# Rotary attention in a four-layer network: the rotation made from the head-padded projections by a VectorE shuffle and GpSimd, and the division moved ahead of the first sums

## The chip, the cores and the metric

The kernel runs on one core of a Trainium2 chip. The metric is the device time of one execution in microseconds. The engines are TensorE (PE; its weight loads are listed as PEld), VectorE (DVE), ScalarE (ACT), GpSimd (POOL) and the queue of SyncE (SP), which issues the transfers.

## The reference

The network takes eight sequences of 256 tokens with 128 features, and runs four layers. Each layer is a feed-forward part (halved and added), an attention part (added) and the same feed-forward part again. All is in float32. The twelve stages are

```python
# layer 0: mixture of experts, softmax attention, mixture of experts
# layer 1: a small projection, an RWKV-6 scan, the small projection
# layer 2: six layers of local attention and MLP, softmax attention, the six layers again
# layer 3: mixture of experts, the attention below, mixture of experts
x = x + _L3_attn_ref(_layernorm(x, axis=-1), L3_attn_Wqkv, L3_attn_Wout, L3_attn_bout)
```

The attention of layer 3, which is the one changed, has 16 heads of 8 features. Its numerator uses rotated queries and keys, its denominator the ones that are not rotated:

```python
def _rotate(t, cos, sin):
    te, to = (t[..., 0::2], t[..., 1::2])
    re = te * cos - to * sin
    ro = te * sin + to * cos
    return jnp.stack([re, ro], axis=-1).reshape(t.shape)

q_rot = _rotate(q, cos, sin)
k_rot = _rotate(k, cos, sin)
num = jnp.exp(jnp.einsum('bhqd,bhkd->bhqk', q_rot, k_rot) * scale)
den = jnp.sum(jnp.exp(jnp.einsum('bhqd,bhkd->bhqk', q, k) * scale), axis=-1, keepdims=True)
attn = jnp.where(causal[None, None], num / den, 0.0)
y = jnp.einsum('bhqk,bhkd->bhqd', attn, v)
return y.transpose(0, 2, 1, 3).reshape(B, C, D) @ Wout + bout
```

## The kernel before

Activations lie as 128 features (partitions) by tokens. The eight sequences are worked in four units of two sequences (`NG = 4`, `T = 512` tokens). A stage takes one unit after the other. What ends a unit and begins its next stage (a residual, a layer norm) is cut into pieces on a queue, and `pump` emits the next piece wherever a stage has a slot for it.

An attention stage works in quads: four heads of one unit, 16 quads in all (4 units x 4 quads). The projections of a quad are padded, so that head j of the quad begins at partition 32 j and has 8 rows there. `attention` runs steps t = 0 to 17. In step t, quad t is projected (`project`), quad t-1 gets its scores and exponentials in four pairs (`pair`: one sequence and two heads each), and quad t-2 is weighed with the values (`weigh`), turned by transposes and divided (`divide`). `before` holds what is made once per unit, and the slots `next(pieces)` and `next(tail)` in a step take pieces: first those of `before` for the next unit, then those of the queue. The last step of a unit also has the `tail`, its output projection.

In attention stages every engine's instructions stay in the order in which the code names them (the class `_Ordered`), so a wait at the head of an engine's queue holds up all that is named later.

PSUM is split three ways. `two(...)` gives a tile of two banks out of three such tiles, which `pp` (projections), `ms` (scores of the rotated) and `ss` (scores of the plain) take in turn. `accp` has one bank for the weighed values (`av`). `ps()` gives the one bank named `bank`, which everything else uses: the values, the transposes of the division, the layer norms, the per-unit products, the output projection. A product into `bank` has to wait until the last reader of what stood in it is done.

In the version before, the rotation is made per unit, in the compact layout. `before` of `attn3` projects queries and keys without padding (`L3_wqk`), copies them (`a_t`), multiplies by a constant matrix of signs (`rot2`) to get the partner of each feature, and forms `a_t * cos` on GpSimd, the partner times sin on VectorE (both `a_y`) and their sum on GpSimd (`a_rot`). For each quad, `project` makes the padded plain projections (`a_qk`), and picks the quad's rotated rows by a product with a selection matrix `sel` (`a_rr`), both copied out of PSUM by VectorE.

`pair` ends with the sums of the plain exponentials (`a_n`) into `q.den`, on VectorE (tile `a_den`). `divide` makes four transposes into `bank`, the reciprocals `a_rec` on VectorE, and the quotient `a_ctx`, which reads `bank`. In the step the division stands behind pair 0:

```python
if q2:
    self.weigh(q2, 1, True)
    self.weighed(q2)        # a_av: VectorE copies av out of PSUM
if q1:
    pair(0, q1)             # scores, a_e and a_n on ACT, a_den on VectorE
if q2:
    self.divide(q2)
next(pieces, None)
```

At the start of the stage GpSimd clears three value buffers (`a_v`, in `value_rows`), one after the other. Both versions have these memsets.

Nearly all instructions of this stage carry the line of the recording helper, L300, in the profile, so they are told apart by their tiles.

Of the kernel before, what the change touches and what calls it, by code (L numbers as in the profile page):

```python
# [24 lines left out]
ALU = mybir.AluOpType  # L25
# [3 lines left out]
P = 128  # L29
B, S, D = 8, 256, 128  # L30
NB = 2
T = NB * S
NG = B // NB
NH = 16
DH = 8
# [17 lines left out]
def _constants():  # L53

    f = np.float32
    p = np.arange(P)
    c = {}
    c["ident"] = np.eye(P, dtype=f)
    c["mean"] = np.full((P, P), 1.0 / P, f)
    c["ones"] = np.ones((P, P), f)  # L60
    c["iota"] = np.tile(np.arange(E, dtype=f), (P, 1))
    c["krow"] = (p % 32 == DH).astype(f)[:, None]
    c["eps"] = np.tile(
        np.array([1e-5, 2e-5, 2.0**-64, 0.5 * SH * math.log(2.0)], f), (P, 1)
    )
    blk = (p[:, None] // 64 == p[None, :] // 64).astype(f)
    c["blkm"] = blk / f(64)

    z = np.zeros((P, 32), f)
    z[:64, :16] = 1.0  # L70
    z[64:, 16:] = 1.0
    c["hsum"] = z
    z = np.zeros((P, 4), f)
    for n, r in enumerate((32, 96, 48, 112)):
        z[r, n] = 1.0
    c["hpick"] = z

    r = np.zeros((P, P), f)
    for m in range(P):
        if m % 2 == 0:  # L80
            r[m + 1, m] = -1.0
        else:
            r[m - 1, m] = 1.0
    c["rot2"] = r

    sel = np.zeros((P, 4, P), f)
    for g in range(4):
        for j in range(4):
            for d in range(DH):
                sel[DH * (4 * g + j) + d, g, 32 * j + d] = 1.0  # L90
    c["sel"] = sel.reshape(P, -1)


    lev = [np.eye(P, dtype=f)]
    for i in range(7):
        n = 2**i
        q = p // n
        lev.append(((q[:, None] % 2 == 0) & (q[None, :] == q[:, None] + 1)).astype(f))
    c["lev"] = np.concatenate(lev, 1)

    c["cq"] = np.where(p[None, :] > p[:, None], f(NEG), f(0))
    c["ck"] = np.where(p[:, None] > p[None, :], f(NEG), f(0))
    one9 = np.zeros((P, 32), f)
    one9[:, DH] = 1.0
    c["one9"] = one9


    i, key = np.arange(32), np.arange(64)
    ok = (key[None, :] >= i[:, None]) & (key[None, :] <= i[:, None] + WIN)
    m = np.zeros((2, 2, 32, 2, 64), f)  # L110
    m[:, 0] = np.where(ok, f(0), f(LNEG))[:, None, :]
    m[:, 1, :, 0, :WIN] = LNEG
    c["lmask"] = m.reshape(P, -1)
    m = np.zeros((2, 2, 32, 4, 32), f)
    m[:, 0] = np.eye(32, dtype=f)[:, None, :]
    m[:, 1, :, 0] = np.eye(32, dtype=f)
    c["lrow"] = m.reshape(P, -1)

    half = np.arange(0, 64, 2, dtype=f)
    inv_freq = f(1.0) / f(10000.0) ** (half / f(64))  # L120
    t = np.arange(S, dtype=f)
    fr = t[:, None] * inv_freq[None, :]
    fr = np.concatenate([fr, fr], -1).T
    base = (half + f(0.4 * 64)) / f(1.4 * 64)
    sc = base[None, :] ** ((t - f(S // 2)) / f(WIN // 2))[:, None]
    sc = np.concatenate([sc, sc], -1).T
    two = lambda a: np.concatenate([_partners(a.T).T] * 2, 0).astype(f)

    sgn = np.where(p[:64, None] < 32, f(-1), f(1))
    c["qcos"] = two(np.cos(fr) * sc * f(8.0))  # L130
    c["qsin"] = two(np.sin(fr) * sc * f(8.0) * sgn)
    c["kcos"] = two(np.cos(fr) * (f(1.0) / sc))
    c["ksin"] = two(np.sin(fr) * (f(1.0) / sc) * sgn)

    i = np.arange(DH // 2, dtype=f)
    th = np.power(f(10000.0), f(-2.0) * (i - f(1.0)) / f(DH))
    ang = t[:, None] * th[None, :]
    per = lambda a: np.tile(np.repeat(a.T, 2, axis=0), (NH, 1)).astype(f)
    c["rcos"] = per(np.cos(ang))
    c["rsin"] = per(np.sin(ang))  # L140

    groups = {
        "c1": ("ident", "mean", "ones", "iota", "krow", "eps"),
        "cs0": ("cq", "ck"),
        "cs1": ("lev", "blkm"),
        "cs2": ("hsum", "hpick", "lmask", "lrow", "qcos", "qsin", "kcos", "ksin"),
        "cs3": ("rot2", "sel", "ck", "one9", "rcos", "rsin"),
    }
    return {n: {k: c[k].astype(f) for k in ks} for n, ks in groups.items()}

# [9 lines left out]
def _partners(w):  # L160

    w = np.asarray(w)
    return w.reshape(w.shape[:-1] + (2, 32)).swapaxes(-1, -2).reshape(w.shape)
# [16 lines left out]
def _layout(inp):  # L180

    g = {k: np.asarray(v) for k, v in inp.items()}
# [56 lines left out]
    for k in ("k", "v", "r", "g", "o"):  # L239
        w1["W" + k] = g["L1_attn_W" + k].T  # L240
    wq = g["L2_attn_w_qkv"]
# [6 lines left out]
    wq = g["L3_attn_Wqkv"]  # L248
    w3 = {
        "L3_wq": _pad_heads(wq[:, :D]),  # L250
        "L3_wk": _pad_heads(wq[:, D : 2 * D]),
        "L3_wqk": wq[:, : 2 * D],
        "L3_wv": wq[:, 2 * D :],
        "L3_wo": g["L3_attn_Wout"],
    }
    a, at = {}, {}
# [9 lines left out]
    w = g["L2_ffn_Wqkv"].reshape(DEPTH, P, 3, 4, 4, 64)  # L266
    w = np.concatenate([_partners(w[:, :, :2]), w[:, :, 2:]], 2)
# [41 lines left out]
class _Net:  # L309
# [582 lines left out]
    def rotated_quads(self):  # L892

        nc = self.nc

        def project(q):
            u = q.unit
            sel = self.get("sel", P * q.g, P)
            q.m = []
            for name, parts in (  # L900
                ("a_qk", ((self.get("L3_wq", P * q.g, P), u.xn), (self.get("L3_wk", P * q.g, P), u.xn))),
                ("a_rr", ((sel, u.rot[0]), (sel, u.rot[1]))),
            ):
                pp = self.two("pp")
                for n, (w, rhs) in enumerate(parts):
                    self.mm(pp[:, n, :], w, rhs)
                t = self.work(name, (P, 2, T), bufs=3)
                nc.vector.tensor_copy(t, pp)
                q.m.append(t)
            q.den = self.work("a_den", (P, 4, 4), bufs=3)  # L910

        def pair(i, q1):
            b, p = i // 2, i % 2
            qk, rr = q1.m
            r, n = self.two("ms"), self.two("ss")
            self.scores([
                (r, rr[:, 1, :], rr[:, 0, :], b, (2 * p, 2 * p + 1), "ck"),
                (n, qk[:, 0, :], qk[:, 1, :], b, (2 - 2 * p, 3 - 2 * p), None),
            ])
            q1.e[b, p] = self.soft(r, 384)  # L920
            e = self.work("a_n", (P, 2, T), bufs=3)
            self.act(e, n, AF.Exp, scale=1.0 / math.sqrt(DH))
            nc.vector.tensor_reduce(
                q1.den[:, 2 * b : 2 * b + 2, 2 - 2 * p : 4 - 2 * p].rearrange("p c j -> p j c"),
                e.rearrange("p j (c k) -> p j c k", c=2), AX.X, ALU.add)

        def step(q0, q1, q2, q3, pieces, tail):
            if q0:
                project(q0)
            else:  # L930
                self.pump()
            if q2:
                self.weigh(q2, 1, True)
                self.weighed(q2)
            if q1:
                pair(0, q1)
            if q2:
                self.divide(q2)
            next(pieces, None)
            if q1:  # L940
                pair(1, q1)
            next(tail if tail else pieces, None)
            if q1:
                pair(2, q1)
                self.weigh(q1, 0, True)
            if tail:
                next(tail, None)
            if q1:
                pair(3, q1)

        return step

# [52 lines left out]

    def attn3(self):
        def before(u):
            nc = self.nc
            self.values(u, self.get("L3_wv"), None)
            yield  # L1010
            u.rot = []
            for i in range(2):
                pp = self.ps()
                self.mm(pp, self.get("L3_wqk", D * i, D), u.xn)
                t = self.work("a_t")
                nc.vector.tensor_copy(t, pp)
                yield
                rp = self.ps()
                self.mm(rp, self.get("rot2"), t)
                seq = lambda a: a.rearrange("p (b s) -> p b s", b=NB)  # L1020
                tab = lambda k: self.get(k).unsqueeze(1).to_broadcast([P, NB, S])
                y1, y2 = self.work("a_y1"), self.work("a_y2")
                nc.gpsimd.tensor_tensor(seq(y1), seq(t), tab("rcos"), ALU.mult)
                nc.vector.tensor_tensor(seq(y2), seq(rp), tab("rsin"), ALU.mult)
                y = self.work(f"a_rot{i}")
                nc.gpsimd.tensor_tensor(y, y1, y2, ALU.add)
                u.rot.append(y)
                yield

        self.attention(self.rotated_quads, before, self.get("L3_wo"), self.get("L3_bout"), 2)  # L1030

# [747 lines left out]
```

## Time and profile before

| | |
|---|---|
| time before, median of 3 runs | 5578.49 us (5568.84 to 5580.77) |
| the profiled execution's own time | 5561.13 us |
| its span, first to last instruction | 5559.4 us |
| mean granted TensorE clock | 0.962 |
| busy: PE, DVE, ACT, POOL | 90%, 63%, 44%, 42% of the span |
| the last attention, from its first `a_v` to its last `x` | about 5085 to 5383 us of the span |

All times of single instructions and waits come from this one profiled execution. A row of a timeline gives the start in us from the span's start, the length in us, the engine, the line, the operation, the tile written and the tiles read, the shape and how many instructions were merged; in brackets stands how long the engine was idle before and what released it. A row of groups ends with busy us and the mean ns of one instruction, and the idle time before with what ended it. A row of waits gives the total, the number of times and the longest. A float32 product of 128x512 shows as two passes.

### The profile page before, as it was taken

What the parts mean: (1) busy time and instruction counts of PE and PEld (TensorE: products, weight loads), DVE (VectorE), ACT (ScalarE), POOL (GpSimd) and SP (SyncE); (2) the same over time, 40 slices, a digit from 0 to 9 for tenths busy, and PEclk for the clock granted to TensorE, in tenths of its full rate; (3) what the DMA queues carried; (4) which work ended last, traced back from release to release, by engine and by line L of the source; (5) the groups of instructions that cost most, each with busy time, mean ns of one, the idle gap of its engine ahead of it and who ended that gap; (6) DMA issues with size and microseconds to landing.
All of it is one profiled execution on the core that took longest, in us unless ns stands there. A gap on an engine that the chain in (4) does not pass through costs nothing.

```text
span 5559.4 us, 161655 instructions
## 1 busy us (share of the span) xinstructions
PE 5031.0 (90%) x73456; PEld 3009.9 (54%) x73456; DVE 3494.9 (63%) x5863; ACT 2440.1 (44%) x2947; POOL 2344.1 (42%) x1205
## 2 busy tenths in 40 slices
PE   9999997899899899988889899989998988899889
PEld 6755754455555555555544455555555555555446
DVE  4444446767767767776645676767767676645555
ACT  2233235444545444444434444545444444433442
POOL 0000022666666666666500666666666666501000
PEclk9999999999999999999989999999999999999999
DMA  1000000111111111111000011111111111000000
GB/s 67 1 1 1 1 1 23 30 35 39 35 40 33 39 34 42 34 35 34 26 23 1 27 38 37 36 40 33 39 34 42 34 35 35 27 34 1 1 1 8
DMA packets 58334, 149.55 MB, mean 27 GB/s; under 512 B 9649, under 2 KB 23858, under 8 KB 57394
## 3 DMA queue, kind: packets, MB, share of 16 engines
q1 hardware_dynamic: 57650, 139.21, 8.3%
q8 instruction: 578, 9.47, 0.7%
q14 instruction: 106, 0.87, 0.1%
HBM read 45.52 MB, written 1.05 MB: 8 GB/s over the span
## 4 chain that ended last, share of the span: by engine, by line
PE 72%; DVE 17%; ACT 6%; issue 4%; POOL 1%; DMA 0%; SPq 0%; DVEq 0%; ACTq 0%; POOLq 0%
PE mm L355 10%; PE pp L300 10%; PE sc L300 7%; PE vp L300 7%; PE e_o L355 6%; PE wo_acc L300 6%; PE bank L300 6%; PE ge L300 5%; DVE l_yr L300 5%; PE cx L300 4%; PE ms L300 3%; PE w_acc L300 2%; DVE l_yk L300 2%; DVE l_yq L300 2%; PE ct L300 2%
## 5 line engine op out<-in xcount | busy, mean ns | idle before, releaser
L300 POOL TENSOR_TENSOR l_yr<-l_yr,l_ksin 128x1024 f32<-128x1024 f32 x192 | 456.8, 2379 | 1024.0 <-DVE l_yr L300 1024.0
L300 PE MATMUL pp<-l_xs,wqkv 128*128 128x512 f32 x1536 | 718.6, 611 | 5.3 <-DMA wqkv<-in_f_wqkv 3.7
L300 ACT COPY l_v<-vp 128x1024 f32<-128x1024 f32 x192 | 194.4, 1013 | 859.3 <-PE vp L300 859.3
L300 ACT ACTIVATE l_sq<-pp 128x1024 f32<-128x1024 f32 x384 | 391.4, 1019 | 283.3 <-PE pp L300 283.3
L300 DVE STREAM_SHUFFLE l_yr<-pp 128x1024 f32<-128x1024 f32 x384 | 505.9, 1318 | 0.0
L300 POOL TENSOR_TENSOR l_e<-l_e,l_rq 128x1024 f32<-128x1024 f32 x192 | 365.7, 1905 | 331.1 <-DVE l_e L300 301.4
L355 PE MATMUL mm<-x,m 128*128 128x512 f32 x1024 | 475.4, 604 | 1.4 <-ACT e_a L387 1.4
L300 DVE TENSOR_REDUCE l_mx<-sc 128x16 f32<-128x1024 f32 x192 | 235.1, 1224 | 374.6 <-PE sc L300 374.6
L300 POOL TENSOR_TENSOR l_yq<-l_yq,l_yr 128x1024 f32<-128x1024 f32 x192 | 456.0, 2375 | 15.0
L300 POOL TENSOR_TENSOR l_yk<-l_yk,l_yr 128x1024 f32<-128x1024 f32 x192 | 453.1, 2360 | 15.1
L300 POOL TENSOR_TENSOR l_yr<-l_yr,l_qsin 128x1024 f32<-128x1024 f32 x192 | 455.1, 2370 | 0.0
L300 PE MATMUL cx<-l_w,l_at 64*32 64x65 f32 x12288 | 304.0, 235 | 148.7 <-ACT l_at L300 123.2
L300 PEld LDWEIGHTS pp<-l_xs,wqkv 128*128 128x128 f32 x1536 | 279.1, 192 | 291.6 <-issue 285.8
L300 PE MATMUL sc<-l_kp,l_yq 64*32 64x64 f32 x24576 | 326.2, 236 | 104.1 <-issue 103.2
L300 PE MATMUL vp<-wqkv,l_xs 128*128 128x256 f32 x1536 | 399.5, 404 | 6.5 <-issue 5.3
L355 PEld LDWEIGHTS e_o<-m,e_h 128*128 128x128 f32 x3072 | 362.9, 192 | 60.6 <-issue 60.1
L300 PEld LDWEIGHTS sc<-l_kp,l_yq 64*32 64x32 f32 x24576 | 277.5, 111 | 172.0 <-issue 170.8
L300 PEld LDWEIGHTS cx<-l_w,l_at 64*32 64x32 f32 x12288 | 261.5, 109 | 197.7 <-ACT l_at L300 137.5
L355 PE MATMUL e_o<-m,e_h 128*128 128x128 f32 x3072 | 363.5, 275 | 0.0
L300 PE MATMUL wo_acc<-l_ct,wo 128*128 128x512 f32 x768 | 358.0, 599 | 0.1
L300 PEld LDWEIGHTS vp<-wqkv,l_xs 128*128 128x128 f32 x1536 | 286.3, 196 | 61.0 <-issue 10.5
L300 PE MATMUL cx<-l_v,l_at 64*32 64x65 f32 x12288 | 309.3, 236 | 6.0 <-issue 6.0
(285 smaller groups left out, 9513.1 us busy)
## 6 DMA issues: line engine op xcount, KB each, us to landing
l_w<-l_v SPq DMA_DIRECT2D x192, 390.0 KB
wqkv<-in_f_wqkv SPq DMA_DIRECT2D x48, 384.0 KB
l_w<-l_v SPq DMA_DIRECT2D x192, 65.0 KB
wo<-in_f_wo SPq DMA_DIRECT2D x12, 512.0 KB
l_rt<-l_rn SPq DMA_DIRECT2D x384, 8.0 KB
m<-in_m_w SPq DMA_DIRECT2D x16, 256.0 KB
w<-in_f_w SPq DMA_DIRECT2D x12, 341.0 KB
w<-in_f_w SPq DMA_DIRECT2D x12, 192.0 KB
```

Of the source, the lines that this page charges most:

```text
L300: r = f(*args, **kw)
L355: self.nc.tensor.matmul(out, lhsT=lhsT, rhs=rhs, start=start, stop=stop)
```

## The change

Four things are edited, all in the last attention.

First, the constants. The matrices `rot2` and `sel` and the unpadded weights `L3_wqk` are no longer loaded. The tables `rcos` and `rsin` now have the padded layout (8 rows in each 32), and the sign of the rotation is in `rsin`.

Second, `before` of `attn3` makes only the values. The two unpadded projections, the two products with `rot2`, their copies and the elementwise operations around them are gone.

Third, `project` makes the rotation for each quad from the padded projections in PSUM: VectorE swaps neighbouring partitions by a shuffle (`a_yr`), VectorE multiplies the projections by cos (`a_rr`), GpSimd multiplies the shuffled ones by the signed sin and adds them onto `a_rr`. The copy of the plain projections (`a_qk`) moves from VectorE to ScalarE. `a_yr` has three buffers, as `a_qk` and `a_rr` have.

Fourth, `pair` returns its sums as a function to be called later. Pairs 1 to 3 call it at once; for pair 0 the step calls it after `divide`, so that on VectorE the division of quad t-2 stands in front of the first sums of quad t-1.

```diff
-        "cs3": ("rot2", "sel", "ck", "one9", "rcos", "rsin"),
+        "cs3": ("ck", "one9", "rcos", "rsin"),
...
         def project(q):
-            u = q.unit
-            sel = self.get("sel", P * q.g, P)
-            q.m = []
-            for name, parts in (
-                ("a_qk", ((self.get("L3_wq", P * q.g, P), u.xn), (self.get("L3_wk", P * q.g, P), u.xn))),
-                ("a_rr", ((sel, u.rot[0]), (sel, u.rot[1]))),
-            ):
-                pp = self.two("pp")
-                for n, (w, rhs) in enumerate(parts):
-                    self.mm(pp[:, n, :], w, rhs)
-                t = self.work(name, (P, 2, T), bufs=3)
-                nc.vector.tensor_copy(t, pp)
-                q.m.append(t)
+            pp = self.two("pp")
+            for n, w in enumerate(("L3_wq", "L3_wk")):
+                self.mm(pp[:, n, :], self.get(w, P * q.g, P), q.unit.xn)
+            qk, rr, yr = (self.work(n, (P, 2, T), bufs=3) for n in ("a_qk", "a_rr", "a_yr"))
+            nc.vector.stream_shuffle(yr, pp, [i ^ 1 for i in range(32)])
+            nc.vector.tensor_tensor(seq(rr), seq(pp), tab("rcos"), ALU.mult)
+            nc.scalar.copy(qk, pp)
+            nc.gpsimd.tensor_tensor(seq(yr), seq(yr), tab("rsin"), ALU.mult)
+            nc.gpsimd.tensor_tensor(rr, rr, yr, ALU.add)
+            q.m = qk, rr
...
-            nc.vector.tensor_reduce(
+            return lambda: nc.vector.tensor_reduce(
                 q1.den[:, 2 * b : 2 * b + 2, 2 - 2 * p : 4 - 2 * p].rearrange("p c j -> p j c"),
...
             if q1:
-                pair(0, q1)
+                sums = pair(0, q1)
             if q2:
                 self.divide(q2)
+            if q1:
+                sums()
             next(pieces, None)
             if q1:
-                pair(1, q1)
+                pair(1, q1)()
...
         def before(u):
             self.values(u, self.get("L3_wv"), None)
             yield
-            u.rot = []
-            for i in range(2):
-                pp = self.ps()
-                self.mm(pp, self.get("L3_wqk", D * i, D), u.xn)
-                t = self.work("a_t")
-                nc.vector.tensor_copy(t, pp)
-                yield
-                rp = self.ps()
-                self.mm(rp, self.get("rot2"), t)
...
-                nc.gpsimd.tensor_tensor(seq(y1), seq(t), tab("rcos"), ALU.mult)
-                nc.vector.tensor_tensor(seq(y2), seq(rp), tab("rsin"), ALU.mult)
-                y = self.work(f"a_rot{i}")
-                nc.gpsimd.tensor_tensor(y, y1, y2, ALU.add)
-                u.rot.append(y)
-                yield
```

More of the change, by code (lines that the diff above doesn't have):

```diff
@@ L76, in _constants @@
     c["hpick"] = z
[L78 to L91, printed above, removed]
     lev = [np.eye(P, dtype=f)]
@@ L137, in _constants, with per @@
     ang = t[:, None] * th[None, :]
-    per = lambda a: np.tile(np.repeat(a.T, 2, axis=0), (NH, 1)).astype(f)
-    c["rcos"] = per(np.cos(ang))
-    c["rsin"] = per(np.sin(ang))
+    def per(a, sgn):
+        z = np.zeros((4, 32, S), f)
+        z[:, :DH] = np.repeat(a.T, 2, axis=0) * sgn[:, None]
+        return z.reshape(P, S)
+    even = np.arange(DH) % 2 == 0
+    c["rcos"] = per(np.cos(ang), np.ones(DH, f))
+    c["rsin"] = per(np.sin(ang), np.where(even, f(-1), f(1)))
     groups = {
@@ L251, in _layout @@
         "L3_wk": _pad_heads(wq[:, D : 2 * D]),
-        "L3_wqk": wq[:, : 2 * D],
         "L3_wv": wq[:, 2 * D :],
@@ L894, in rotated_quads @@
         nc = self.nc
+        seq = lambda a: a.rearrange("p n (b s) -> p (n b) s", b=NB)
+        tab = lambda k: self.get(k).unsqueeze(1).to_broadcast([P, 2 * NB, S])
         def project(q):
-            u = q.unit
-            sel = self.get("sel", P * q.g, P)
-            q.m = []
-            for name, parts in (
-                ("a_qk", ((self.get("L3_wq", P * q.g, P), u.xn), (self.get("L3_wk", P * q.g, P), u.xn))),
-                ("a_rr", ((sel, u.rot[0]), (sel, u.rot[1]))),
-            ):
-                pp = self.two("pp")
-                for n, (w, rhs) in enumerate(parts):
-                    self.mm(pp[:, n, :], w, rhs)
-                t = self.work(name, (P, 2, T), bufs=3)
-                nc.vector.tensor_copy(t, pp)
-                q.m.append(t)
+            pp = self.two("pp")
[8 more added lines that the diff above has]
+            q.m = qk, rr
             q.den = self.work("a_den", (P, 4, 4), bufs=3)
@@ L935, in step @@
             if q1:
-                pair(0, q1)
+                sums = pair(0, q1)
             if q2:
                 self.divide(q2)
+            if q1:
+                sums()
             next(pieces, None)
             if q1:
-                pair(1, q1)
+                pair(1, q1)()
             next(tail if tail else pieces, None)
             if q1:
-                pair(2, q1)
+                pair(2, q1)()
                 self.weigh(q1, 0, True)
@@ L948, in step @@
             if q1:
-                pair(3, q1)
+                pair(3, q1)()
         return step
@@ L1007, in before @@
         def before(u):
-            nc = self.nc
             self.values(u, self.get("L3_wv"), None)
             yield
-            u.rot = []
-            for i in range(2):
-                pp = self.ps()
-                self.mm(pp, self.get("L3_wqk", D * i, D), u.xn)
-                t = self.work("a_t")
-                nc.vector.tensor_copy(t, pp)
-                yield
-                rp = self.ps()
-                self.mm(rp, self.get("rot2"), t)
-                seq = lambda a: a.rearrange("p (b s) -> p b s", b=NB)
-                tab = lambda k: self.get(k).unsqueeze(1).to_broadcast([P, NB, S])
-                y1, y2 = self.work("a_y1"), self.work("a_y2")
-                nc.gpsimd.tensor_tensor(seq(y1), seq(t), tab("rcos"), ALU.mult)
-                nc.vector.tensor_tensor(seq(y2), seq(rp), tab("rsin"), ALU.mult)
-                y = self.work(f"a_rot{i}")
-                nc.gpsimd.tensor_tensor(y, y1, y2, ALU.add)
-                u.rot.append(y)
-                yield
         self.attention(self.rotated_quads, before, self.get("L3_wo"), self.get("L3_bout"), 2)
```

## The prediction

> **What bounds the kernel now.** I read the page first, for the whole program.
>
> ```profile
> span 5559.4 us, 161655 instructions
> PE 5031.0 (90%) x73456; PEld 3009.9 (54%) x73456; DVE 3494.9 (63%) x5863; ACT 2440.1 (44%) x2947; POOL 2344.1 (42%) x1205
> ```
>
> TensorE is busy for 90% of the span, but that average runs over twelve stages. The change touches the last attention only. By its tiles that runs from 5085 us (first `a_v`) to 5383 us (last `x`): about 298 us, 5.4% of the span. Nothing outside can move, apart from two constant loads that get smaller (0.46 MB of 149.55 MB, landed long before). So the second view is the waits, and the third the groups by shape, both from 5090 to 5385 us.
>
> ```profile
> ACT a_e L300 <- PE ms L300: 154.3, 52, 29.5
> DVE a_den L300 <- ACT a_n L300: 93.0, 59, 3.1
> PEld bank L300 <- DVE a_ctx L300: 39.4, 14, 3.1
> PE bank L300 <- DVE a_ctx L300: 35.6, 14, 2.8
> ```
>
> ```profile
> L300 PE MATMUL pp<-a_rot,sb_cs 128*128 128x512 f32 x64 | 30.1, 592 | 0.0
> L300 PE MATMUL bank<-a_t,sb_cs 128*128 128x512 f32 x16 | 14.4, 997 | 10.1 <-DVE a_ctx L300 8.5 <-issue 0.8 <-DVE a_t L300 0.8
> ```
>
> ACT and DVE mostly wait for others, so PE is the bound, and PE has one large wait of its own: 14 times, 35.6 us in all, it stands before a product into `bank`, because the division (`a_ctx`) has not yet read that one PSUM bank. The timeline of a step shows why.
>
> ```profile
> 5119.73 1.98 PE L300 MATMUL pp<-x,sb_w 128*128 128x512 f32 x4
> 5121.39 1.22 DVE L300 TENSOR_REDUCE a_den<-a_n 128x4 f32<-128x1024 f32 x1 [0.97 <-ACT a_n L300]
> 5121.56 1.88 PE L300 MATMUL pp<-a_rot,sb_cs 128*128 128x512 f32 x4
> 5122.52 1.21 DVE L300 COPY a_qk<-pp 128x1024 f32<-128x1024 f32 x1
> 5123.65 1.21 DVE L300 COPY a_rr<-pp 128x1024 f32<-128x1024 f32 x1
> 5124.78 0.68 DVE L300 COPY a_av<-av 128x512 f32<-128x512 f32 x1
> 5125.55 0.66 PE L300 MATMUL bank<-sb_c,a_av 128*128 128x128 f32 x4
> 5127.20 1.22 DVE L300 TENSOR_REDUCE a_den<-a_n 128x4 f32<-128x1024 f32 x1 [1.74 <-ACT a_n L300]
> 5128.69 0.29 DVE L300 TENSOR_TENSOR a_ctx<-bank,a_rec 128x128 f32<-128x128 f32 x1
> 5129.03 2.08 PE L300 MATMUL bank<-a_t,sb_cs 128*128 128x512 f32 x2 [2.82 <-DVE a_ctx L300]
> ```
>
> The transposes end at 5126.2, but DVE's queue has the sums of pair 0 (`a_den`, which needs ACT's exponential) in front of the division, so PE idles 2.82 us. The first product after it took 2.08 us for two passes, against 1.12 at other places: the clock had dropped.
>
> **The change part by part.** I count from the start of `pp` in a step (5119.73 is 0). Where two DVE rows follow each other, the distance of their starts counts (1.13 us for a 128x1024 copy).
>
> *Division ahead of the first sums.* The division no longer waits for `a_n`. Behind `a_av` come `a_rec` (0.24) and `a_ctx` (0.29), which needs the end of the transposes; then the sums. PE resumes some 0.1 us after `a_ctx`. The sums of pair 0 are read only by the next step's division, and `a_n` has three buffers: nothing is late by them.
>
> *The products of the rotation.* Per quad two selection products go (4 passes, 0.43 us each: 1.71 us), per unit two projections and two rotations (3.43 us); 16 x 1.71 + 4 x 3.43 = 41 us of PE. Not all of this lies on the path. In the step above PE reaches the transposes when DVE has made `a_av`, and that stands behind `a_den` of pair 3 and two 128x1024 passes. With the change the two passes are a shuffle and a product, which the long local stage already runs in this shape. Groups of the page (busy us, mean ns):
>
> ```profile
> L300 DVE STREAM_SHUFFLE l_yr<-pp 128x1024 f32<-128x1024 f32 x384 | 505.9, 1318 | 0.0
> L300 POOL TENSOR_TENSOR l_yr<-l_yr,l_qsin 128x1024 f32<-128x1024 f32 x192 | 455.1, 2370 | 0.0
> ```
>
> and, by tile (shortest, median and longest ns),
>
> ```profile
> L300 DVE TENSOR_TENSOR l_yq<-pp,l_qcos x192: 1193/1206/1225, 970.2 to 4833.4; 128x1024 f32<-128x1024 f32 x192
> L300 ACT COPY l_v<-vp x192: 1012/1012/1016, 975.0 to 4845.2; 128x1024 f32<-128x1024 f32 x192
> ```
>
> So DVE runs `a_den` 1.66, shuffle 2.79, product 4.00 (the local stage has 1.21 from a shuffle's start to the next row's), `a_av` 5.13 to 5.81; transposes at 5.90 instead of 5.82. PE, meanwhile, needs 1.71 for `pp`, 0.79 for the weighing, 1.40 for pair 0, and stands ready at 3.90. **The 1.71 us saved on the selection turn into a new 2.0 us wait for `a_av`**; this term is -0.08 x 14 = -1.1 us. After the transposes: `a_ctx` ends at about 6.9, PE resumes at 7.0 instead of 9.30 if a product into `bank` is next, else goes on with pair 1 at 6.40. In the new order of PE, a product into `bank` follows the division directly in 6 of the 14 steps (fewer pieces are left to spread), each waiting about 0.6 us. So of 35.6 us about 3.6 stay: **+32.0 us**.
>
> *Pieces.* From the third step on, nine of the per-unit products (the last of unit 1, all of units 2 and 3) go: 9 x 0.86 = **+7.7 us**; their copies on DVE (`a_t`, `a_y`, 0.69 each) were off the path.
>
> *The start.* Before, unit 0's chain of product, copy, product, product runs with nothing beside it, and pair 0 begins at 5110.24. Now the first `pp` can start when the values' products end (5085.42). DVE first copies `a_v` (done 5088.55, behind POOL's first memset), then shuffle and product to 5091.0; POOL's three memsets (5.34 us from 5085.98) end at 5091.3, then 2.38 + 2.36 for the two POOL passes: rotated projections at 5096.1, pair 0 at 5096.2. That is 14 us earlier; I take off 1 us since PE stands idle from about 5092 and begins at half clock. **+13 us**.
>
> *What is added beside the path.* ACT copies `qk` at about 2.0 to 3.0; its last exponential ends at 1.62 and the next, queued behind the copy, cannot start before 3.80, so it costs nothing; without that gap it would be 1.0 us a step. POOL makes 2 x 2.37 after the shuffle (4.1): `rr` is ready at about 8.9, and its first reader is pair 0 of the next step, at 11.9 + 2.5 = 14.4, since a step without pieces comes to about 11.9 us. Nothing else is queued on POOL. The PSUM buffer of `pp` is read until 5.1 and taken again by pair 1 at 6.40. SP only issues the two smaller loads.
>
> [...] *Clock.* Windows of 1 us around that step give
>
> ```profile
> 5128.00:5129.00 1.00, 0.00 (x0) 0.00 (x0) 0.88 (x3) 0.00 (x0) 0.00 (x0) 0.95 0.00 0
> 5129.00:5130.00 1.00, 0.97 (x1) 0.50 (x2) 0.00 (x0) 0.00 (x0) 0.00 (x0) 0.50 0.00 0
> 5132.00:5133.00 1.00, 1.00 (x17) 0.59 (x10) 0.00 (x0) 0.16 (x1) 0.95 (x1) 0.84 0.00 0
> ```
>
> (the seventh number is the granted clock). After a gap of 2.82 us the clock is 0.50 for about 3.4 us. Of three gaps of 1.53 us (ending at 5220.3, 5288.8 and 5302.7) the last did it, the others not. [...] The new gap of 2.0 us (then 0.6 more in six steps) lies nearer to 2.82 than to no gap, so I expect about as many cold windows as before: 0, with bounds of +15 and -5 (three more windows, 1.7 us each).
>
> [...]
>
> **Sum.** 32.0 + 7.7 + 13 - 1.1 = 51.6; I say 52. The profiled execution took 5561.1 us (its span and 1.7); the median shown is 5578.5, 0.3% longer. The same difference on the median: **5526 us**.
>
> **Rivals.**
> - *Clock kept.* If 2.0 us gaps leave the clock alone, 52 + 15 = 67: 5511 us. For it: one 1.53 us gap did nothing; and two more like it; against: eleven 2.82 us gaps, nearly all cooled. Chance 0.20.
> - *Start or pieces give less.* If the first steps stay cold, or layer norms queue behind the moved sums and PE waits for `bank` there, some 20 us of the gain go: 5546 us. Chance 0.17.
> - *Slower: POOL late.* If GpSimd's two passes were held up so that `rr` comes after 14.4, every pair 0 waits. The point is 4.1 + 2p = 14.4, p = 5.1 us a pass against 2.37 measured; to lose the whole gain and 11 us over 15 steps, lateness must reach 4.2 us: p = 7.3. At p = 8 it is 5.8 x 15 = 87 - 52 = 35 us slower: 5613 us. [...] Chance, with the unforeseen, 0.06.
> - *No visible change.* The gains eaten by new waits, 5570 to 5590: 0.04.
>
> The forecast itself has 0.53. About 0.2% (11 us) is what a measurement of this kernel can tell from no change; its three runs lie 12 us apart. Faster 0.90, same 0.04, slower 0.06. The range takes in the clock's bound with some run noise below and the small-gain case above: 5499 to 5549.
>
> **What would show it.** Right: waits for `a_ctx` at a few us; a wait of PE for `a_av` near 2.0 us in most steps, about 28 us in all; `ms<-a_rr` first at about 5096; the stage about 246 us long; granted clock there still 0.90 to 0.93. Wrong: waits of `ms` for POOL `a_rr` after the first step; `a_yr` on POOL above 5 us; a granted clock near 1.0 (more gain), or shuffles far from 1.32 us.

## The result, and the profile after

The changed kernel takes 5523.26 us (median of four runs, 5514.1 to 5532.29), and the kernel before 5573.66 us over the runs beside it. The ratio is 0.9913, with a 95% interval of 0.9891 to 0.9935: about 50 us faster, where 52 were forecast.

The page of the changed kernel begins:

```profile
span 5524.2 us, 161509 instructions
PE 5007.5 (91%) x73360; PEld 3006.1 (54%) x73360; DVE 3489.0 (63%) x5863; ACT 2452.8 (44%) x2963; POOL 2396.6 (43%) x1221
```

The two profiled spans differ by 35 us only. To see why, I take the stage by itself, from GpSimd's first clearing of `a_v` to the end of the last `x<-bank,sb_pv,x`. Before it runs from 5085.98 to 5383.52 (297.5 us), after from 5102.38 to 5348.22 (245.8 us): **51.7 us shorter**. What follows takes 176 us in both. What comes before the stage took 16.4 us longer in this one execution, though its instructions are the same in both kernels. So executions differ elsewhere by such amounts, and the stage is the sharper measure. I give it for each experiment, beside the runs. It comes from one profiled execution per kernel; two executions of the changed kernel gave 245.8 and 242.7 us. In experiments 1, 2, 3, 5 and 6 the interval of the runs' ratio overlaps with that of the changed kernel, so there the difference from the changed kernel rests on the stage.

PE's wait for `a_av` in the stage before (total, times, longest):

```profile
PE bank L300 <- DVE a_av L300: 2.4, 2, 1.9
```

The waits of the stage after the change (5103 to 5348 us):

```profile
ACT a_qk L290 <- DVE a_rr L290: 62.3, 16, 9.0
PE bank L290 <- DVE a_av L290: 25.5, 16, 1.9
PE ms L290 <- POOL a_rr L290: 4.4, 1, 4.4
PE bank L290 <- DVE a_ctx L290: 2.3, 6, 0.4
```

The 35.6 us for `a_ctx` have gone to 2.3. In their place stands `a_av` with 25.5, where it had 2.4 before, and GpSimd's result is waited for once, at the very start. A step of the timeline has the same order of events that the prediction walked through:

```profile
5210.81 1.98 PE L290 MATMUL pp<-x,sb_w 128*128 128x512 f32 x4
5212.47 1.22 DVE L290 TENSOR_REDUCE a_den<-a_n 128x4 f32<-128x1024 f32 x1 [2.24 <-ACT a_n L290]
5213.61 1.30 DVE L290 STREAM_SHUFFLE a_yr<-pp 128x1024 f32<-128x1024 f32 x1
5214.80 1.21 DVE L290 TENSOR_TENSOR a_rr<-pp,sb_cs 128x1024 f32<-128x1024 f32 x1
5215.92 0.68 DVE L290 COPY a_av<-av 128x512 f32<-128x512 f32 x1
5216.10 1.01 ACT L290 COPY a_qk<-pp 128x1024 f32<-128x1024 f32 x1 [3.67 <-DVE a_rr L290]
5216.66 1.02 PE L290 MATMUL bank<-sb_c,a_av 128*128 128x128 f32 x4 [1.69 <-DVE a_av L290]
5217.73 0.29 DVE L290 TENSOR_TENSOR a_ctx<-bank,a_rec 128x128 f32<-128x128 f32 x1 [0.96 <-PE bank L290]
5218.07 2.07 PE L290 MATMUL bank<-sb_w,x 128*128 128x128 f32 x8 [0.39 <-DVE a_ctx L290]
5218.77 1.22 DVE L290 TENSOR_REDUCE a_den<-a_n 128x4 f32<-128x1024 f32 x1 [0.76 <-ACT a_n L290]
```

Counted from `pp`, the shuffle begins at 2.80 (forecast 2.79), the cosine product at 3.99 (4.00), `a_av` at 5.11 (5.13), the transposes at 5.85 (5.90). PE resumes at 7.26 (7.0). One row is not where it was put: ScalarE copies `qk` at 5.29 instead of 2.0: it stands idle for 3.67 us until VectorE's `a_rr` is done, which reads the same PSUM tile. Experiment 6 asks what that costs.

Groups of the stage after (busy us, mean ns) show that the added passes cost what the local stage had shown:

```profile
L290 POOL TENSOR_TENSOR a_rr<-a_rr,a_yr 128x1024 f32<-128x1024 f32 x16 | 37.6, 2353 | 1.3
L290 DVE STREAM_SHUFFLE a_yr<-pp 128x1024 f32<-128x1024 f32 x16 | 20.8, 1299 | 0.0
L290 DVE TENSOR_TENSOR a_rr<-pp,sb_cs 128x1024 f32<-128x1024 f32 x16 | 19.3, 1208 | 0.0
L290 ACT COPY a_qk<-pp 128x1024 f32<-128x1024 f32 x16 | 16.2, 1012 | 62.3 <-DVE a_rr L290 62.3
```

Last, the windows over the stage (length, busy PE, PEld, DVE, ACT, POOL, then the granted clock, DMA share, GB/s), of before

```profile
5086.00:5383.00 297.00, 248.94 (x1969) 127.97 (x1970) 155.34 (x182) 118.64 (x142) 25.62 (x19) 0.90 0.00 1
```

and of after:

```profile
5103.00:5348.00 245.00, 206.49 (x1873) 113.49 (x1872) 145.53 (x181) 133.33 (x158) 79.90 (x35) 0.88 0.00 1
```

Read in slices of 0.2 us, the stage after the change has a clock of 1.00 or 0.50 in 1208 of 1230 slices; the other values stand where it changes. So a mean of 0.90 over 297 us is about 60 us at half clock, and 0.88 over 245 us is 59. The change left that amount as it was. This number decides most of what follows.

### The profile page after: what moved, and what is told of

It reads as the page before. It is cut to its first block, busy times and chain, and to the rows that moved or that the text cites. A ratio compares the mean times of both kernels' runs of the same rounds, so it can differ in the third digit from the quotient of the medians.

```text
span 5524.2 us, 161509 instructions
## 1 busy us (share of the span) xinstructions
PE 5007.5 (91%) x73360; PEld 3006.1 (54%) x73360; DVE 3489.0 (63%) x5863; ACT 2452.8 (44%) x2963; POOL 2396.6 (43%) x1221
## 4 chain that ended last, share of the span: by engine, by line
PE 71%; DVE 17%; ACT 6%; issue 4%; POOL 1%; DMA 0%; DVEq 0%; SPq 0%; POOLq 0%; ACTq 0%
PE mm L345 10%; PE pp L290 9%; PE vp L290 7%; PE sc L290 7%; PE e_o L345 6%; PE wo_acc L290 6%; PE bank L290 5%; PE ge L290 5%; DVE l_yr L290 4%; PE cx L290 4%; PE ms L290 2%; PE w_acc L290 2%; DVE l_yk L290 2%; PE ct L290 2%; DVE l_yq L290 2%
```

## The experiments

My theory has three parts. VectorE's queue, not TensorE's work, sets when a step goes on. Where TensorE is made to stand still for some 1.7 us in each step, the clock falls to half for 3.41 or 6.83 us (in the stage after it is at half for no other length), so a gap costs more than its length. GpSimd's passes are hidden. The rivals are that the removed TensorE work is the gain, that ScalarE's new wait lies on the path, and that the clock does not mind such gaps.

### 1. The division edit alone

```diff
 # the kernel before, and only this of the change:
-                pair(0, q1)
+                sums = pair(0, q1)
             if q2:
                 self.divide(q2)
+            if q1:
+                sums()
```

> The kernel before with the fourth edit alone (sums of pair 0 behind the division). My theory: the 14 waits of PE for a_ctx (35.6 us) shrink to about 0.6 us each, since the transposes still end near 6.5 us of a step and a_ctx then follows at once: 27 us off, and the clock about as it was; stage (first values product to last x) 298 to about 271 us. Rival (the products are what counts, the wait only moves to the next thing, ACT or PSUM): under 10 us off, other waits of PE grow by what a_ctx loses. Second rival (with the 2.8 us gaps gone, the clock also stays up): 27 + 15 = 42 us off.

Measured: 5512.44 us against 5556.58 for the kernel before on this chip, ratio 0.9913 (0.9898 to 0.9928); the stage 250.4 us, 47 shorter. Its wait for `a_ctx`, and its windows:

```profile
PE bank L300 <- DVE a_ctx L300: 4.2, 11, 0.4
...
PE bank L300 <- DVE a_av L300: 2.4, 2, 1.9
```

```profile
5073.00:5322.00 249.00, 230.89 (x1969) 118.84 (x1970) 154.43 (x181) 117.71 (x142) 24.85 (x19) 0.97 0.00 1
```

The second rival holds. The wait shrank by 31 us, and the clock rose from 0.90 to 0.97 as well, from about 60 to 15 us at half clock. One call moved behind another, with no work removed, gives 47 of the 52 us that the whole change gives, and by the runs the same ratio.

### 2. The rotation alone

```diff
 # the changed kernel, with the sums of pair 0 called at once:
-                sums = pair(0, q1)
+                pair(0, q1)()
             if q2:
                 self.divide(q2)
-            if q1:
-                sums()
```

> The changed kernel with the sums of pair 0 called at once, in front of the division: edits one to three alone. My theory: the start keeps its 12 us and the pieces their 8; the wait for a_av stays near 1.7 us a step; but the division comes behind a_n again, which is now late (ACT copies qk at 5.3 and makes a_n until 8.0), so a_ctx ends at about 9.7 and the six steps with a product into bank behind the division wait 2.5 us and more, and the tails' transposes too: about 20 us of the 50 go, 30 off against before. The two edits alone (27 + 30) then give about what both give together. Rival (all gain is from removed TensorE work, the division edit adds nothing): 50 off, as the changed kernel.

Measured: 5523.2 against 5556.58, ratio 0.9938 (0.9925 to 0.9952); the stage 266.2 us, 31 shorter than before, as expected. PE now has both waits, and the lowest clock so far:

```profile
PE bank L290 <- DVE a_av L290: 25.5, 16, 1.9
PE bank L290 <- DVE a_ctx L290: 21.4, 9, 3.3
```

```profile
5080.00:5345.00 265.00, 212.04 (x1873) 116.18 (x1872) 145.53 (x181) 133.33 (x158) 79.55 (x35) 0.84 0.00 1
```

The stage gains 47 by the one part, 31 by the other, and 52 by both. So the parts do not add. Against the kernel with the division edit alone, the rotation brings only 5 to 8 us more (250.4 to 245.8 and 242.7), which the runs do not show, though it takes 41 us of TensorE work away: it also brings the wait for `a_av`, and with it the low clock.

### 3. One more VectorE pass in front of `a_av`

```diff
-            nc.scalar.copy(qk, pp)
+            nc.vector.tensor_copy(qk, pp)
```

> The changed kernel with the copy of the plain projections back on VectorE, behind shuffle and cosine product: one more pass of 1.13 us in front of a_av. My theory (VectorE's chain a_den, shuffle, product, a_av sets when the transposes start): PE's wait for a_av grows from 1.7 to 2.8 us, 14 to 15 steps x 1.1 = 16 us slower than the changed kernel, with the clock a little lower. Rival (ScalarE, which now waits for VectorE before it copies, is the bound): moving the copy off ScalarE makes it no slower or faster.

Measured: 5525.79 against 5556.58, ratio 0.994 (0.9925 to 0.9956); the stage 263.6 us, 18 longer than the changed kernel's (16 expected).

```profile
PE bank L290 <- DVE a_av L290: 41.1, 16, 2.8
```

```profile
5077.00:5340.00 263.00, 212.42 (x1874) 115.81 (x1873) 162.51 (x197) 118.60 (x142) 80.21 (x35) 0.85 0.00 1
```

The wait grew from 25.5 to 41.1 us. This is VectorE's chain, seen from the other side: the 16 passes of 1.13 us in front of `a_av`, 18 us in all, are paid in full. The clock fell from 0.88 to 0.85, but little is left over that it could have cost. ScalarE was relieved of the copy and that helped nothing.

### 4. Useless products in the gap

```diff
         tp = self.ps()
+        if q.den is not None:
+            for _ in range(4):
+                self.mm(tp[:, :S], self.get("ident"), self.get("rcos"))
         for c in range(4):
```

> The changed kernel with four useless products (each 128x256, two passes, 1.7 us in all at full clock) into the bank of the transposes just in front of them, where PE otherwise waits some 1.7 us for a_av; what they write is overwritten. My theory (gaps of 1.7 us cool the clock for a window of 3.4 us or two): the granted clock in the steps rises from 0.89 to over 0.95, and the stage gets 10 to 18 us shorter though it does more work. [...]

Measured: 5494.64 against 5556.58, ratio 0.9871 (0.9852 to 0.989); the stage 227.4 us, 18 shorter than the changed kernel's.

```profile
5068.00:5294.00 226.00, 212.57 (x2001) 126.49 (x2000) 145.07 (x181) 131.84 (x158) 79.78 (x35) 0.98 0.00 1
```

With the gap filled, no wait for `a_av` is left and the clock is 0.98; the 7 us at half clock that remain lie at the start, where TensorE waits for the first `a_rr`. TensorE does 128 passes more than in the changed kernel (2001 against 1873 rows) and is done earlier. Gaps of 1.7 us in steps of some 14 us were therefore enough to pull the clock down. What a gap must be like to do it stands in the last section.

### 5. The slower rival: GpSimd late

Useless passes were put between GpSimd's sine product and its sum; they write a tile that nobody reads.

```diff
+            extra = self.work("a_extra", (P, 2, T), bufs=1)
+            for _ in range(4):          # 8 in the second of the two kernels
+                nc.gpsimd.tensor_tensor(extra, yr, yr, ALU.add)
             nc.gpsimd.tensor_tensor(rr, rr, yr, ALU.add)
```

With four:

> The changed kernel with four useless GpSimd passes of 128x1024 (a sum into a tile that nobody reads) between the sine product and the sum of each quad. My theory (GpSimd is hidden until its chain is longer than a step and the weighing of the next one): the chain is 4.1 + 6 x 2.4 = 18.5 us in a step where rr is needed at about 14.4 at the earliest, and six passes are 14.4 us a quad, which is the step itself: each step grows to about 16 to 18 us, 25 to 55 us slower than the changed kernel. With this the point from which the slower rival decides is placed. Rival (GpSimd has room enough, or is late already): no change, or 9.6 x 15 = 144 us slower.

Measured: 5533.17 against 5570.76, ratio 0.9933 (0.9917 to 0.9948). The changed kernel beside it on the same chip had 0.9928 (0.9915 to 0.9941), so no difference. The stage took 253.0 us against 242.7 there, and 7.6 us of this lie in the first steps, before anything overlaps. My theory missed here. GpSimd's `a_rr` is waited for six times, 18.6 us in all, but 12.2 of them at the start, where the changed kernel waits 4.4. A useless pass took about 1.9 us instead of the 2.4 that I used, so the chain ends at 4.1 + 2.35 + 7.8 + 2.36 = 16.6 us. And a step of 14.5 us, longer than the one without pieces, needs `rr` only at about 17.

With eight:

> The changed kernel with eight useless GpSimd passes per quad in place of four. A useless pass measured 1.95 us, so a quad keeps GpSimd for 2 x 2.35 + 8 x 1.95 = 20.3 us. My theory (four cost nothing because the chain of 16.6 us still ended before the next step's first rotated scores at about 17): now GpSimd is the bound, all steps become 20.3 us long, and the stage about 247 + 14 x 6 + 16 = 347 us, 100 us slower than the changed kernel: slower than before. Rival (hidden further on): under 30 us slower.

Measured: 5620.04 against 5562.98, ratio 1.0097 (1.0077 to 1.0118); the stage 351.9 us (347 expected).

```profile
PE ms L290 <- POOL a_rr L290: 123.6, 16, 20.0
```

Now GpSimd is the bound and the kernel is slower than before. The slower rival is a real mechanism, but its point lies far off: with a chain of 16.6 us it cost next to nothing, and the change needs 4.1 + 4.7 = 8.8. The changed kernel itself, run beside the first of these:

> The changed kernel itself, to stand beside the others on one chip: 0.991 of before, stage about 247 us, some 58 us of it at half clock.

Measured: 5532.67 against 5570.76, the stage 242.7 us with a granted clock of 0.89, some 51 us of it at half clock where 58 were expected.

### 6. ScalarE's copy first

```diff
+            nc.scalar.copy(qk, pp)
             nc.vector.stream_shuffle(yr, pp, [i ^ 1 for i in range(32)])
             nc.vector.tensor_tensor(seq(rr), seq(pp), tab("rcos"), ALU.mult)
-            nc.scalar.copy(qk, pp)
```

> The changed kernel with the copy of the plain projections named in front of the shuffle, so that ScalarE need not wait for VectorE (62 us of waiting in all in the changed kernel). My theory: ScalarE is no bound there; its exponential of pair 0 starts at 3.8 instead of 6.2 us, while VectorE's shuffle waits for the copy, 3.1 instead of 2.8: transposes 0.3 us later, the steps with few pieces a little shorter: within 5 us of the changed kernel. Rival (the 62 us lie on the path): 20 us or more faster.

Measured: 5521.1 against 5570.76, ratio 0.9913 (0.9899 to 0.9928); the stage 246.4 us, where the changed kernel had 245.8 and 242.7. ScalarE no longer waits for VectorE before this copy, so the edit did what it should; PE's wait for `a_av` went from 25.5 to 31.1 us. The stage is the same within what it varies; the runs alone could hold a small gain. The 62 us that ScalarE waited were not on the path.

### 7. The rotation behind `a_av`

If VectorE's two passes in front of `a_av` are the bound, they belong behind it. This version copies `qk` first and names the rotation later:

```diff
 # project: pp, then nc.scalar.copy(qk, pp); rotation in two functions
+            def cosines():
+                nc.vector.tensor_tensor(seq(rr), seq(qk), tab("rcos"), ALU.mult)
+            def sines():
+                nc.vector.stream_shuffle(yr, qk, [i ^ 1 for i in range(32)])
+                nc.gpsimd.tensor_tensor(seq(yr), seq(yr), tab("rsin"), ALU.mult)
+                nc.gpsimd.tensor_tensor(rr, rr, yr, ALU.add)
 # step: cosines() behind weighed(q2), sines() behind divide(q2), then sums()
```

> The changed kernel with the copy qk first and the rotation taken from this copy in SBUF, behind a_av on VectorE: cosine product behind a_av, shuffle behind the division. My theory (the wait for a_av is VectorE's two passes standing in front of it, and the clock drops by that gap): a_av at 2.8, transposes at 3.9, no gap left; a step without pieces takes about 10 instead of 12 us, the half-clock time falls to about that of the division alone (17 us): stage about 247 - 14 x 1.7 - 20 = 203 us, at the least under 225. rr is then ready at about 11 us and is needed at 12. Rivals: the cosine product with two SBUF operands is held up by GpSimd and the late shuffle makes pair 0 wait for rr: stage about as before, 240 us or more.

Measured: 5484.68 against 5570.76, ratio 0.9839 (0.9822 to 0.9856); the stage 204.8 us (203 expected), 41 shorter than the changed kernel's. Its waits and its windows:

```profile
PE ms L290 <- POOL a_rr L290: 5.5, 1, 5.5
...
PE bank L290 <- DVE a_ctx L290: 3.1, 6, 0.5
PE bank L290 <- DVE a_av L290: 2.4, 2, 1.9
```

```profile
5106.00:5310.00 204.00, 185.34 (x1873) 102.80 (x1872) 147.41 (x181) 133.67 (x158) 81.81 (x35) 0.97 0.01 1
```

The same operations as in the changed kernel, on the same engines, in another order, and with the rotation reading the copy in SBUF in place of PSUM: `a_av` is waited for 2.4 us instead of 25.5, and the clock is 0.97. A step without pieces went from 12.0 to 10.0 us.

### 8. The same order, read from PSUM

```diff
-                nc.vector.tensor_tensor(seq(rr), seq(qk), tab("rcos"), ALU.mult)
+                nc.vector.tensor_tensor(seq(rr), seq(pp), tab("rcos"), ALU.mult)
-                nc.vector.stream_shuffle(yr, qk, [i ^ 1 for i in range(32)])
+                nc.vector.stream_shuffle(yr, pp, [i ^ 1 for i in range(32)])
```

> The kernel with the rotation behind a_av, but with cosine product and shuffle reading the projections in PSUM as in the changed kernel, instead of the copy in SBUF. It tells apart the two halves of that version. My theory: the tile pp is then read until the shuffle ends, near 6.3 us of a step, while pair 1 wants its PSUM buffer at 4.4: the wait for a_av comes back as a wait of about 1.9 us for this buffer, and the clock drops by it: stage 235 to 250 us. Rival (the place behind a_av is all that counts): stage about 206 us, as with the copy in SBUF.

Measured: 5466.99 against 5562.98, ratio 0.983 (0.9806 to 0.9854); the stage 206.6 us. The rival holds: where the rotation reads makes no difference that shows, and the copy named first gained nothing by itself (experiment 6), so the place behind `a_av` is what counts. My reason for a new wait was wrong. I had pair 1 take the buffer of `pp`, the three being used in turn, as the prediction had it too. The timeline has pair 1 begin its first product into `ms` at 5169.34, while `pp` still has its shuffle to come:

```profile
5168.48 0.81 ACT L290 ACTIVATE a_e<-ms 128x768 f32<-128x768 f32 x1 [0.96 <-PE ms L290]
...
5169.34 0.38 PE L290 MATMUL ms<-low_ck,low_ident 128*128 128x256 bf16 x2
...
5169.62 1.30 DVE L290 STREAM_SHUFFLE a_yr<-pp 128x1024 f32<-128x1024 f32 x1
```

so pair 1 has another buffer. It begins 0.05 us after ScalarE has read the `ms` of pair 0, so that one is the likely buffer, and the three are not taken strictly in turn. Versions 7 and 8 beat both kernels, by a ratio of 0.983 to 0.984 to the one before; between them nothing is told apart.

## Why the prediction was right, point by point

The forecast for the stage was 51.6 us shorter; it is 51.7. That close a match is luck: two executions of the changed kernel lie 3.1 us apart in the stage. The terms:

- *Division, +32.0.* The wait went from 35.6 to 2.3 us, that is 33.3.
- *The selection products turn into a wait, -1.1.* Right, and it is the main reading. The wait for `a_av` came, 25.5 us in all where about 28 were forecast, 1.6 to 1.7 us in most steps where 2.0 were: in the step shown TensorE stood ready at 4.16 instead of 3.90.
- *The start, +13.* The first rotated scores came 11.75 us after the first values product (5112.51 and 5100.76) instead of about 26, and the third step's `pp` about 12.4 us earlier.
- *Pieces, +7.7.* Not measured alone. From the third step's `pp` to the end the stage is 39.3 us shorter, where division, selection and pieces together were forecast at 38.6.
- *GpSimd and ScalarE beside the path.* GpSimd as forecast. ScalarE's copy was put at the wrong place: in all 16 quads it began only after VectorE's product had read the same PSUM tile, and it waited 62.3 us in all; in experiment 8, where the copy is named first and VectorE's product reads the same tile, the product waited for the copy twice, 1.0 us in all. The prediction had the copy start at 2.0 with nothing to wait for. The wait cost nothing (experiment 6).
- *The clock, 0.* Right in size: 60 us at half clock before, 59 after. Summed by slices it is 61 and 58 us, of which 14 and 7 lie at the start of the stage; in the steps it rose from 48 to 51 us, within the bound of 5. The 15 us of the bound above, which the rival *Clock kept* adds, and the second rival of experiment 1 too, were an estimate that no row or run shows. What the runs showed of a clock that stays up is 16 us beyond the wait in experiment 1 (mean clock 0.97) and 18 us in experiment 4, which shows by its clock of 0.98 that the gaps were the cause.
- *What the sum hid.* The terms read as though the division edit were worth 32 us and the rotation some 20. By experiments 1 and 2 the division edit alone is worth 47 and the rotation alone 31. The clock term came out at 0 because the one part freed the clock and the other took it again. The prediction never asked what each edit would do to the clock by itself.
- *The slower rival* was priced from 14.4 us, the shortest step. Experiment 5 shows that the usual step leaves until about 17. (At 8 us a pass the lateness is 5.7 us, not 5.8, which changes the price by 1.5 us.)

Not settled: why the unchanged stages differ between executions. Up to the start of this one they took 5067 to 5079 us on one chip, 5083 to 5089 on a second and 5098 to 5112 on a third, and TensorE was busy there for 4604 to 4610, 4609 to 4617 and 4624 to 4637 us with the same products. So the difference goes with the chip and with TensorE's pace; what makes the pace is open.

## What to carry to other kernels

Before removing work from the engine that bounds a stage, ask which queue the engine meets next. Here 1.7 us of TensorE work a step became 1.7 us of waiting, since VectorE's two passes stood in front of the copy that TensorE needed. Where every engine runs in order, the first thing to try is to name the instruction that another engine waits for ahead of the ones that nobody waits for yet. And count the clock with each gap: a short gap that comes back in every step can cost more than itself (experiment 1: 47 us for 31 us of waits), and filling or closing it can be worth more than work that is saved (18 and 41 us in experiments 4 and 7, against 5 to 8 for the rotation added to the division edit).

## What the hardware showed that was not expected

- Gaps of 1.6 to 1.7 us, one in nearly every step of about 14 us, held TensorE at half clock for some 51 of 245 us; with the gaps filled by useless products the mean clock was 0.98.
- Not each gap did it, and its length alone did not decide. In each of the twelve profiles of this stage the clock changes only at points that lie whole multiples of 3.41 us apart. So I cut each stage into these stretches of 3.41 us, took those at full clock, and sorted them by how long TensorE stood still within them:

| TensorE stood still within a stretch | stretches | the next one at half clock |
|---|---|---|
| under 1.0 us | 546 | 1 |
| 1.0 to 1.5 us | 40 | 2 |
| 1.5 to 2.0 us | 50 | 41 |
| over 2.0 us | 63 | 63 |

So in these profiles the sum of standing still within one stretch told what came next, with the border near 1.5 us. A gap of 1.7 us that two stretches share could pass: in the changed kernel the one of 1.68 us that ended at 5245.14 lay across the border of two stretches at 5244.11, with 1.42 us of standing still in the second, and the clock stayed at 1.00. In the changed kernel 10 of the 16 waits for `a_av` were followed by half clock, and of the prediction's three gaps of 1.53 us, right at the border, one was.

- Half-clock time had no steady price. The division edit alone took about 45 us of it away, and the stage lost 47 - 31 = 16 us beyond the wait; the filler took about 50 away, and the stage lost 18 us without any less work in it. Both give about 0.35 us for each us at half clock. But experiments 2 and 3 added 26 and 20 us at half clock, and the stage grew by only 1 and 2 us more than the waits did.
- In experiment 7's kernel, where the cosine product reads two SBUF operands, one of VectorE's 16 products took 2.35 us where the median is 1.22, and one of GpSimd's 16 sums 3.22 where the median is 2.36. Read from PSUM, in the changed kernel, the longest of the 16 products took 1.22 us. In the local stage before, `l_kp`, which reads two SBUF operands too, has a median of 1.23 and a longest of 2.40. What held them up is not shown. The first rotated scores came 11.2 us after the start of the stage; in experiment 8's kernel, which reads PSUM, they came after 10.3, about 1 us earlier (shortest, median and longest ns, in experiment 7's kernel):

```profile
L290 DVE TENSOR_TENSOR a_rr<-a_qk,sb_cs x16: 1212/1215/2352, 5108.8 to 5282.5; 128x1024 f32<-128x1024 f32 x16
L290 POOL TENSOR_TENSOR a_rr<-a_rr,a_yr x16: 2347/2357/3216, 5113.8 to 5288.0; 128x1024 f32<-128x1024 f32 x16
```
